# Places of a chunk without an edge: from a fetch of row 0 to no fetch, in a sparse graph-attention kernel

## The chip, the cores and the metric

The kernel runs on one core of one Trainium2 chip. The metric is the device time of one execution in microseconds (us). A second source is the hardware profile of one further execution, with every instruction, its waits and the packets of the DMA engines.

## The reference

Two layers of graph attention over 4096 nodes with 512 features. The adjacency is sparse: a random matrix of zeros and ones whose density falls with the index of both nodes, so that early nodes have many edges and late ones few. In this input there are 33,143 edges, and 15 nodes without any. Cut to what matters:

```python
# layer 0
h  = einsum('nf,kfp->knp', x, W);  f1, f2 = h . a_src, h . a_dst        # 8 heads of 64
e  = where(adj > 0, leaky_relu(f2[:, :, None] + f1[:, None, :], 0.2), -1e16)
x  = layernorm(x + concat_heads(softmax(e) @ h))
# layer 1: the same with 8 heads, elu, then the same with one head of 512, elu,
# then relu(out @ lin1_w + lin1_b) @ lin2_w + lin2_b
x  = layernorm(x + ...)
```

So attention is computed three times over the same edges: stage 0 (8 heads), stage 1 (8 heads) and stage 2 (one head of 512). A node without an edge gets the mean of all rows.

## The kernel before

**Edge search.** For each of 32 tiles of 128 nodes, `find_edges` reads the adjacency rows, finds the columns of the edges with VectorE's max operations, and writes them as a list of places. The places of one half of a tile (64 nodes) lie one after another, 128 to a chunk, one place on each partition. The number of chunks is fixed when the program is built, from the expected number of edges with a margin of 4.2 standard deviations; a pair is one chunk of each half. A place has three things: `idx`, the row to fetch (L926); `nl`, which of the 64 nodes it belongs to, or -1 if it holds no edge (L904); and its column in `s1`, from which TensorE spreads the node's score over the places. For a place without an edge, `idx` comes out as 0 and its column of `s1` as zeros. Tile 0 has four parts and more than 100 candidates a part and goes another way (L917 on). The blocks of `find_edges` are put in order by a scheduler; what follows is in an order written out by hand.

**Stages 0 and 1** (`heads_layer`) go over the tiles from 31 down to 0, in units of up to six chunks. `Attention.gather` issues one indirect DMA per chunk on GpSimd's queue (L987): each partition gets the table row (520 floats: features and a score for each head) that `idx` names. The gathers write into buffers `g` of six chunks; seven of these are in use (GB), so GpSimd runs seven units ahead and waits only for a buffer that TensorE has finished with. `spread` multiplies `s1` with the node's score split into three bf16 parts (L1013), and VectorE adds these up (L1022). `weights` adds the fetched score (L1052 to L1054) and takes the exponential on ScalarE, once in place in `g` (L1056) and once to scale the rows (L1059). `add` makes the selection matrix `sm` by comparing `nl` with 0 to 63 (L1080), scales the rows (L1111) and accumulates `sm` times rows on TensorE (L1102). A place with `nl` of -1 has an empty row in `sm`, so what it fetched counts for nothing. In the hand-written order, `weights` of the next unit stands before `add` of this one. When a tile is done it is normalised and projected to the next stage's table, which SP's queue writes to HBM (L681); at the end comes one more row, the mean (`finish_mean`, L740). The next stage's gathers wait for the whole table.

**Stage 2** has four buffers (GT), rows of 514 floats, the weight inside `sm` (L1089), and two dense layers (L1376, L1388) that are woven in between units by a fixed pace.

Lines that the text below touches: L904 (`nl`), L916 and L922 (`src`), L926 (`idx`), L852 to L875 (the degrees of a tile), L882 (`s1`), L987 (gather), L1009 to L1026 (scores), L1190 (first gathers of stages 0 and 1), L1326 (first gathers of stage 2).

Of the kernel before, what the change touches and what calls it, by code (L numbers as in the profile page):

```python
# [10 lines left out]
F32 = mybir.dt.float32  # L11
BF16 = mybir.dt.bfloat16
# [3 lines left out]
AF = mybir.ActivationFunctionType  # L16
OP = mybir.AluOpType
# [4 lines left out]
P = 128  # L22
N = 4096
F = 512
# [13 lines left out]
HS = 8  # L38
DM = 64
HN = P // 2  # L40
GC = 6
GB = 7
KW = 512
WIDE = 12
GT = 4

# [488 lines left out]
def sparse_path(  # L535
# [23 lines left out]
    nc = tc.nc  # L559
# [3 lines left out]
    total = sum(p.pairs for p in pts)  # L563
# [26 lines left out]

    idx = const.tile([P, total, 2], I32, name="idx")
    nl = const.tile([P, total, 2], F32, name="nl")
    s1 = const.tile([P, total * P], BF16, name="s1")

    class Stage2:
# [198 lines left out]
    def find_edges(big, sb, ps, pk, constants, sg, beside):  # L794
# [10 lines left out]
        for v, p in enumerate(pts):  # L805
# [89 lines left out]
            for lo in range(0, nch, per):  # L895
                m = min(per, nch - lo)
                pl = ps.tile([P, m, 2, k + 2], F32, name="pl")
                for c in range(m):
                    chunk = s1[:, (c0 + lo + c) * P : (c0 + lo + c + 1) * P]
                    nc.tensor.matmul(pl[:, c], chunk, rhs, start=True, stop=False)  # L900
                    nc.tensor.matmul(pl[:, c, :, : k + 1], chunk, rest, start=False, stop=False)
                    nc.tensor.matmul(pl[:, c, :, k:], ident_b, own_b, start=False, stop=True)
                cs = slice(c0 + lo, c0 + lo + m)
                nc.scalar.copy(nl[:, cs], pl[:, :, :, k + 1])  # L904
                src = sb.tile([P, most * 2], F32, name="src")[:, : 2 * m]
                sel = sb.tile([P, 512], F32, name="sel")[:, : m * 2 * k].rearrange("p (m h k) -> p m h k", k=k, h=2)
                if k < 100:
                    shape = [P, m, 2, k]
                    nc.vector.tensor_tensor(
                        sel,  # L910
                        iota_k[:, lo : lo + m, None, :k].to_broadcast(shape),
                        pl[:, :, :, k : k + 1].to_broadcast(shape),
                        op=OP.is_equal,
                    )
                    nc.vector.tensor_tensor(sel, sel, pl[:, :, :, :k], op=OP.mult)
                    nc.vector.tensor_reduce(src, sel.rearrange("p m h k -> p (m h) k"), AX.X, OP.add)  # L916
                else:  # L917
                    kk = sb.tile([P, most, 2], F32, name="kk")[:, :m]
                    nc.scalar.copy(kk, pl[:, :, :, k])
                    for c in range(m):  # L920
                        for h in range(2):
                            nc.vector.scalar_tensor_tensor(  # L922
                                sel[:, c, h], iota_k[:, lo + c, :k], kk[:, c, h : h + 1], pl[:, c, h, :k],
                                op0=OP.is_equal, op1=OP.mult, accum_out=src[:, 2 * c + h : 2 * c + h + 1],
                            )
                nc.gpsimd.tensor_copy(idx[:, cs].rearrange("p m h -> p (m h)"), src)  # L926
            if p.last:
                beside(t)
        limits = [big.tile([P, nv], F32, name=f"limits{i}") for i in range(2)]
# [46 lines left out]
    class Attention:  # L976
# [4 lines left out]
            self.s, self.ls, self.acc, self.den, self.seen = {}, {}, {}, {}, {}  # L981

        def gather(self, u):
            u.g = self.gp.tile([P, GC, F + HS], F32, name="g")
            for k in range(u.n):
                i, h = divmod(k, u.hn)
                nc.gpsimd.indirect_dma_start(  # L987
                    out=u.g[:, k, : self.st.row],
                    out_offset=None,
                    in_=self.st.table[:, :],  # L990
                    in_offset=bass.IndirectOffsetOnAxis(ap=idx[:, u.c0 + i, h : h + 1], axis=0),
                    bounds_check=N,
                    oob_is_err=False,
                )

        def spread(self, t):
# [5 lines left out]
            for name, of in (("s", self.s), ("ls", self.ls)):  # L1002
# [1 line left out]
                    [P, widest if wide else WIDE, 2, hs], F32, name=f"{name}{hs}",  # L1004
                    tag=f"{name}w" if wide else name, bufs=1 if wide else 3,
                )[:, :pairs]
            cuts = list(range(0, pairs, 10))

            def scores(lo):  # L1009
                pss = self.ps.tile([P, 10, 2, 3, hs], F32, name="pss")  # L1010
                m = min(10, pairs - lo)
                for i in range(m):
                    nc.tensor.matmul(  # L1013
                        pss[:, i].rearrange("p g a h -> p (g a h)"),
                        s1[:, ts(base + lo + i, P)],
                        st.s3[:, t].rearrange("p g a h -> p (g a h)"),
                        start=True, stop=True,
                    )
                return pss[:, :m]

# [153 lines left out]

        return rest

    def heads_layer(gp, wk, sb, pp, st, nxt, fetch, finish):

# [3 lines left out]
        with tc.tile_pool(name=f"ha_{st.name}", bufs=2, space=PSUM, reuse_waits="tile") as pacc, \  # L1184
# [2 lines left out]
                tc.manual_schedule():  # L1187
            at = Attention(st, gp, wk, pacc, one)
            extra = {}
            for u in units[:GB]:  # L1190
                at.gather(u)
            for t in order[:2]:
# [109 lines left out]

        return rest

    heads_layer(gp, wk, sb, pp, st0, st1, fetch0, finish0)
    heads_layer(gp, wk, sb, pp, st1, st2, lambda t: None, lambda o, t, _: elu(sb, o))


    layers.close()
    with tc.tile_pool(name="tg", bufs=GT, side="right", reuse_waits="tile") as gp, \  # L1310
# [12 lines left out]
        order = [t for block in blocks for t in block]  # L1323
        units = units_of(order)
        at = Attention(st2, gp, wk, pacc, ps)
        for u in units[:GT]:  # L1326
            at.gather(u)
        l1w = big.tile([P, FC, HID], F32, name="sl1w")
# [167 lines left out]
```

## Time and profile before

| | |
|---|---|
| median of six executions | 2272.0 us (2269.53 to 2275.16) |
| the profiled execution | 2275.27 us, of which the span of instructions is 2273.5 us |
| edge search, up to the first gather | 0 to 524 us |
| stage 0, first gather to first gather of the next | 524.3 to 1012.2 us |
| stage 1 | 1012.2 to 1497.4 us |
| stage 2 | 1497.4 us to the end |
| busy: TensorE, VectorE, ScalarE, GpSimd | 1741.7, 1362.3, 650.6, 1214.9 us |
| gathers | 1017, 1031.9 us busy on GpSimd, 1015 ns mean |
| DMA | 139,788 packets, 415.47 MB, of these 81,360 packets and 269.79 MB for the gathers |
| granted TensorE clock, mean | 0.895 |

Reading it: the busy time of a gather is GpSimd's own work on it; when the rows land is seen from what waits for them. A wait is listed under the engine and line that waited, with what released it. Shares over the whole span mix four phases with different limits, so the phases are looked at one by one.

### The profile page before, as it was taken

How to read it: one execution, taken by the hardware profiler on the slowest of the kernel's cores; microseconds unless marked ns; L12 is line 12 of the kernel's file. 1: busy time of each engine (PE TensorE's matmuls, PEld its weight loads, DVE VectorE, ACT ScalarE, POOL GpSimd, SP SyncE). 2: the span in 40 equal slices, each digit the busy share in tenths (PEclk: the TensorE clock that was granted, in tenths of full speed). 3: DMA queues.
4: the chain of work that ended last, by engine and by line, in shares of the span. 5: the costliest groups of instructions: out<-in, count | busy, mean ns of one | idle time of the engine just before them, and what ended most of it. 6: DMA issues, size and time to landing. Idle time of an engine off the chain costs nothing.

```text
span 2273.5 us, 29407 instructions
## 1 busy us (share of the span) xinstructions
PE 1741.7 (77%) x8935; PEld 1019.2 (45%) x8935; DVE 1362.3 (60%) x3744; ACT 650.6 (29%) x2354; POOL 1214.9 (53%) x1647
## 2 busy tenths in 40 slices
PE   3887876662887876756987767638989998898987
PEld 2665532221655553424655444325444444444444
DVE  5787777774989987736877667524242433424322
ACT  3346766560332221102433222012111111111111
POOL 5413333336777777727777777555547544444300
PEclk9899987785999997877999997869999999999998
DMA  6434555536998988727888888575556645544401
GB/s 213 126 112 162 201 202 219 216 118 169 282 276 275 276 260 235 222 80 213 234 224 224 224 216 216 156 214 162 148 152 189 187 127 150 159 129 145 134 19 43
DMA packets 139788, 415.47 MB, mean 183 GB/s; under 512 B 33819, under 2 KB 34851, under 8 KB 135654
## 3 DMA queue, kind: packets, MB, share of 16 engines
q0 software_dynamic: 81360, 269.79, 43.6%
q1 hardware_dynamic: 58262, 143.72, 18.0%
q8 instruction: 74, 1.21, 0.2%
q14 instruction: 92, 0.75, 0.1%
HBM read 371.18 MB, written 42.24 MB: 182 GB/s over the span
## 4 chain that ended last, share of the span: by engine, by line
PE 22%; DMA 13%; issue 13%; DVE 12%; POOL 9%; ACT 1%; POOLq 0%; DVEq 0%; SPq 0%; ACTq 0%
DMA g<-table_t,idx 11%; PE p L1376 10%; POOL g L987 9%; PE acc L1102 7%; DVE g L1111 4%; PE p L1388 3%; PE ph L667 2%; DMA xr<-sx_d 2%; DVE bs L1160 1%; DVE sm L1089 1%; DVE xr L1393 1%; DVE sm L1080 1%; DVE z L1053 1%; DVE z L1052 1%; DVE o L1139 1%
## 5 line engine op out<-in xcount | busy, mean ns | idle before, releaser
L987 POOL DMA_INDIRECT g<-table_t,idx x1017 | 1031.9, 1015 | 600.1 <-issue 296.4
L1102 PE MATMUL acc<-g,sm 128*64 128x260 f32 (+2 forms) x4068 | 602.6, 432 | 268.6 <-DVE g L1111 194.9
L1102 PEld LDWEIGHTS acc<-g,sm 128*64 128x64 f32 x4068 | 344.9, 153 | 498.9 <-DVE g L1111 253.7
L667 PE MATMUL ph<-sw_t,xt 128*128 128x264 f32 (+1 forms) x1536 | 392.0, 404 | 49.7 <-ACT xt L656 39.2
L1111 DVE TENSOR_TENSOR g<-g,wp 128x2048 f32<-128x2048 f32 (+4 forms) x148 | 383.2, 2589 | 10.6 <-ACT wp L1059 10.6
L667 PEld LDWEIGHTS ph<-sw_t,xt 128*128 128x128 f32 x1536 | 292.5, 197 | 114.3 <-ACT xt L656 55.4
L825 DVE MAX8 cand<-key 128x8 f32<-128x24 f32 (+54 forms) x467 | 196.7, 445 | 83.4 <-PE key L819 83.1
L1388 PE MATMUL p<-sl2w,shid 128*128 128x512 f32 x512 | 229.5, 602 | 0.0
L1376 PE MATMUL p<-sht,sl1w 128*128 128x512 f32 (+1 forms) x576 | 227.9, 551 | 0.0
L1052 DVE TENSOR_TENSOR z<-s,g 128x48 f32<-128x48 f32 (+6 forms) x222 | 40.8, 184 | 240.8 <-DMA g<-table_t,idx 231.5
L656 ACT ACTIVATE xt<-pt 128x128 f32<-128x128 f32 x384 | 101.4, 279 | 218.5 <-PE pt L653 217.9
L1376 PEld LDWEIGHTS p<-sht,sl1w 128*128 128x128 f32 x576 | 107.6, 191 | 110.4 <-issue 105.5
L1388 PEld LDWEIGHTS p<-sl2w,shid 128*128 128x128 f32 x512 | 96.0, 192 | 121.0 <-issue 120.5
L818 PE MATMUL key<-sg,s_identb 128*128 128x512 bf16 (+1 forms) x258 | 116.1, 451 | 30.1 <-DVE cand L825 25.5
L791 ACT ACTIVATE sg<-raw 128x4096 bf16<-128x4096 int32 (+1 forms) x39 | 116.9, 2998 | 9.8 <-PE key L818 5.0
L680 ACT COPY hrow<-ph 128x260 f32<-128x260 f32 (+2 forms) x194 | 70.7, 373 | 169.9 <-PE ph L667 169.9
L819 PE MATMUL key<-frac,places 128*128 128x512 bf16 (+1 forms) x258 | 116.7, 453 | 1.8 <-POOL places L754 1.8
L1379 ACT ACTIVATE shid<-p,sl1b 128x512 f32<-128x512 f32 (+1 forms) x72 | 46.1, 640 | 248.7 <-PE p L1376 248.7
L1089 DVE TENSOR_SCALAR sm<-iota_n,nl,w 128x64 f32<-128x64 f32 x339 | 83.8, 325 | 46.1 <-ACT w L1062 45.8
L1156 DVE SCALAR_TENSOR_TENSOR o<-ex,o 128x512 f32<-128x512 f32 x64 | 44.1, 689 | 100.3 <-ACT ex L1155 100.2
L1059 ACT ACTIVATE wp<-z 128x32 f32<-128x32 f32 (+4 forms) x148 | 30.6, 207 | 236.9 <-DVE g L1111 236.8
L852 POOL TENSOR_SCALAR degs<-balance 128x1 f32<-128x1 f32 x35 | 6.7, 192 | 141.8 <-ACT signs L850 137.3
(161 smaller groups left out, 1830.1 us busy)
## 6 DMA issues: line engine op xcount, KB each, us to landing
raw<-in_adj_dram SPq DMA_DIRECT2D x31, 2048.0 KB, 7.7
table_t<-hrow SPq DMA_DIRECT2D x64, 260.0 KB, 4.0
xr<-in_x_dram SPq DMA_DIRECT2D x64, 256.0 KB, 4.1
g<-table_t,idx POOLq DMA_INDIRECT x1017
table_t<-hrow SPq DMA_DIRECT2D x32, 257.0 KB, 5.5
sx_d<-o SPq DMA_DIRECT2D x32, 256.0 KB, 5.1
xr<-sx_d SPq DMA_DIRECT2D x32, 256.0 KB
out_dram<-xr SPq DMA_DIRECT2D x32, 256.0 KB, 3.0
```

Source lines behind the costliest of these rows:

```text
L656: nc.scalar.activation(xt[:, c, :], pt[:, c, :], AF.Copy, accum_out=st.xparts[:, c, t : t + 1])
L667: nc.tensor.matmul(ph[:n], columns(c), st.w[:, c, j], start=(c == 0), stop=(c == FC - 1))
L791: nc.scalar.activation(sg[:, ts(i, w)], raw[:, ts(i, w)], AF.Sign)
L818: nc.tensor.matmul(out_, ident_b, sg[:, j:e], start=True, stop=False)
L819: nc.tensor.matmul(out_, places[:, w], frac[:, j - w * KW : e - w * KW], start=False, stop=True)
L825: nc.vector.max(out=cand[:, at : at + 8], in_=part)
L987: nc.gpsimd.indirect_dma_start(out=u.g[:, k, : self.st.row], out_offset=None, in_=self.st.table[:, :], in_offset=bass.IndirectOffsetOnAxis ...
L1089: nc.vector.tensor_scalar(sm[:, k], iota_n, node[:, i, h : h + 1], u.w[:, k], op0=OP.is_equal, op1=OP.mult)
L1102: nc.tensor.matmul(out_[h * HN : (h + 1) * HN], sm[:, k], rows(k), start=flags[k][0], stop=flags[k][1])
L1111: nc.vector.tensor_mul(body, body, wp[:, :, :, None].to_broadcast(body.shape))
L1376: nc.tensor.matmul(p1, l1w[:, c, ts(k, P)], hts[b][:, c, :n], start=(c == 0), stop=(c == FC - 1))
L1388: nc.tensor.matmul(p2, hids[b][:, k, ts(j, P)], l2w[:, k, :], start=(k == 0), stop=(k == HC - 1))
```

## The change

A place without an edge gets a row number past the table's end: `past` is 8192 where `nl` is below -0.5 and 0 elsewhere, and is added to `src` before the cast to `idx`. The gather's bound is 4096 (`bounds_check=N`), and a row past it is to be left out without an error (`oob_is_err=False`); both were there before. What such a place finds in its buffer is then what was there earlier. So that this is a finite number, the buffers are filled with zeros once: seven passes of ScalarE ahead of stage 0's gathers, none for stage 1, which has the same buffers, and four memsets on GpSimd ahead of stage 2's gathers, whose buffers lie elsewhere in memory. So that the exponential stays finite as well, the score of such a place becomes -1e30: `hole` holds this value, and one more matmul per group of pairs puts it beside the three parts of the score, in a fourth column that VectorE's sum takes in. The sum less its own leaky value is then 0, and the weight 1. Groups of scores go from ten pairs to eight, so that a group with four parts still fits its PSUM tile.

```diff
+FAR = -1e30
+    hole = const.tile([P, total, 2], BF16, name="hole")
...
                 nc.scalar.copy(nl[:, cs], pl[:, :, :, k + 1])
+                nc.gpsimd.tensor_scalar(hole[:, cs], nl[:, cs], -0.5, FAR, op0=OP.is_lt, op1=OP.mult)
...
-                nc.gpsimd.tensor_copy(idx[:, cs].rearrange("p m h -> p (m h)"), src)
+                past = sb.tile([P, most * 2], F32, name="past")[:, : 2 * m]
+                nc.gpsimd.tensor_scalar(
+                    past, nl[:, cs].rearrange("p m h -> p (m h)"), -0.5, 2.0 * N, op0=OP.is_lt, op1=OP.mult
+                )
+                nc.gpsimd.tensor_add(past, past, src)
+                nc.gpsimd.tensor_copy(idx[:, cs].rearrange("p m h -> p (m h)"), past)
...
-            cuts = list(range(0, pairs, 10))
+            cuts = list(range(0, pairs, 8))
...
-                pss = self.ps.tile([P, 10, 2, 3, hs], F32, name="pss")
-                m = min(10, pairs - lo)
+                pss = self.ps.tile([P, 8, 2, 4, hs], F32, name="pss")
+                m = min(8, pairs - lo)
+                nc.tensor.matmul(
+                    pss[:, :m, :, 3, :], ident_b,
+                    hole[:, base + lo : base + lo + m, :, None].to_broadcast([P, m, 2, hs]),
+                    start=True, stop=True,
+                )
                 for i in range(m):
                     nc.tensor.matmul(
-                        pss[:, i].rearrange("p g a h -> p (g a h)"),
-                        s1[:, ts(base + lo + i, P)],
-                        st.s3[:, t].rearrange("p g a h -> p (g a h)"),
-                        start=True, stop=True,
+                        pss[:, i, :, :3, :], s1[:, ts(base + lo + i, P)], st.s3[:, t], start=True, stop=True
                     )
...
             at = Attention(st, gp, wk, pacc, one)
             extra = {}
+            if clear:
+                for _ in range(GB):
+                    g = gp.tile([P, GC * (F + HS)], F32, name="g")
+                    nc.scalar.activation(g, ones.to_broadcast(g.shape), AF.Copy, scale=0.0)
             for u in units[:GB]:
                 at.gather(u)
...
-    heads_layer(gp, wk, sb, pp, st0, st1, fetch0, finish0)
-    heads_layer(gp, wk, sb, pp, st1, st2, lambda t: None, lambda o, t, _: elu(sb, o))
+    heads_layer(gp, wk, sb, pp, st0, st1, fetch0, finish0, True)
+    heads_layer(gp, wk, sb, pp, st1, st2, lambda t: None, lambda o, t, _: elu(sb, o), False)
...
         at = Attention(st2, gp, wk, pacc, ps)
+        for _ in range(GT):
+            nc.gpsimd.memset(gp.tile([P, GC, F + HS], F32, name="g"), 0.0)
         for u in units[:GT]:
             at.gather(u)
```

## The prediction

> **What bounds the kernel now.** I read the page's busy shares and slices first, then busy time by stretch, then the gathers' group and the GpSimd waits, then GpSimd in order of time, then the DMA queues.
>
> ```profile
> POOL 5413333336777777727777777555547544444300
> DMA  6434555536998988727888888575556645544401
> ```
> The two rows of the 40 slices: from slice 11 (568 us) both GpSimd and the DMA engines are busy for most of the two eight-head stages, DMA more so. By stretch (busy us and count for each engine, clock, DMA share, GB/s):
>
> ```profile
> core 0: us, PE busy (x) PEld busy (x) DVE busy (x) ACT busy (x) POOL busy (x), PEclk, DMA share, GB/s
> 620.00:973.00 353.00, 273.07 (x1726) 178.13 (x1725) 301.25 (x585) 81.87 (x472) 267.80 (x266) 0.92 0.86 257
> 1064.00:1460.00 396.00, 309.38 (x1957) 205.05 (x1955) 288.51 (x492) 114.02 (x544) 304.83 (x300) 0.91 0.83 222
> 1497.00:2273.00 776.00, 672.93 (x2747) 352.07 (x2745) 269.29 (x978) 129.56 (x306) 343.49 (x339) 0.94 0.48 137
> ```
> No engine looks full in the first two; the third stage is TensorE's (673 of 776). What paces the first two shows only in GpSimd's waits (520 to 1480 us: releaser, us in total, times, longest):
>
> ```profile
> POOL g L987 <- issue: 213.9, 577, 37.6
> ```
> and in its order of time (start, us, what, idle before):
>
> ```profile
> 528.52 1.00 POOL L987 DMA_INDIRECT g<-table_t,idx  x1 [0.30 <-issue]
> 529.82 1.00 POOL L987 DMA_INDIRECT g<-table_t,idx  x1 [0.31 <-issue]
> ...
> 1459.79 1.00 POOL L987 DMA_INDIRECT g<-table_t,idx  x1 [0.30 <-issue]
> 1497.44 1.00 POOL L987 DMA_INDIRECT g<-table_t,idx  x1 [36.65 <-PE pss L1013]
> ```
> Each gather is 1.00 us of descriptor work and 0.30 us in which GpSimd waits for nothing shown. I took the distance of all neighbours: in both stages the median is 1.304 us, and only 10 of 338 (stage 0) and 15 of 338 (stage 1) exceed 1.5 us, 6.4 and 5.0 us of excess together. 338 x 1.304 = 441 us of the 449.3 and 447.6 us from first gather to last. So GpSimd's issue of gathers sets the pace of stages 0 and 1; DMA at 86% is a follower. In stage 2 gathers wait for TensorE to free buffers (213 us of waits on the accumulating matmuls there).
>
> ```profile
> q0 software_dynamic: 81360, 269.79, 43.6%
> ```
> All gathers: 81,360 packets are 1017 x 80, 64 of two rows and 16 completions of 4 B for every gather, whatever its places hold.
>
> From the inputs I counted the places: 339 gathers x 128 = 43,392 a stage, against 33,143 edges and 15 nodes without one. So 10,234 (23.6%) are empty; 42 gathers are empty throughout, 68 partly. All these fetch row 0, and the trace shows it: matching packets to gathers by order, a packet of a full gather takes 212 ns (stage 0) and 232 (stage 1), of an all-empty one 331 and 342; from end of issue to landing 3.2 and 3.0 us against 4.3 and 4.0. GpSimd's own time does not differ: 1.011 and 1.002 us in stage 0.
>
> **What the Trainium skill says.** "Perfetto Trace Analysis", DMA Instruction — SWDGE (GPSIMD): the profiled end of such a DMA is when the last DSP has generated descriptors, not when data has moved. The trace agrees: landing comes 3 us later. So the 1.00 us is generation, and fewer bytes don't shorten it. "DMA: Bandwidth & Descriptors", Why a DMA increments its semaphore by 16: for SWDGE all 16 engines post their count whatever the shape; the 16 small packets agree, so an empty gather still completes. "GPSIMD Engine Reference", 3.1: data-dependent branching costs about 12 cycles an element (10 ns at the page's 1.2 GHz). No run here shows what a row past the bound costs; that price is my upper end.
>
> **The change, part by part.** Sums are made against the profiled execution (2275.27 us, span 2273.5), which lies 3.3 us above the median of the six runs, 2272.0.
>
> 1. *Rows not fetched.* Per stage 10,234 x 2080 B = 21 MB less. In stages 0 and 1 this is hidden behind GpSimd's 1.304 us a gather: 0, if generation stays at 1.00 us. Unknown: the time of a place past the bound. Ends: nothing at all, -7.8 ns (1000/128), and +10 ns (the skill's branch). A gather has 30 such places on average. I take 0, since generation is one steady figure now (995 to 1000 ns for the 5th to 50th percentile) and the bound is already tested for every row.
>
> 2. *Earlier landing at the two stage ends*, which are on the path: after the last gather everything waits for it. The last unit of stages 0 and 1 holds 128, 128, 21 and 0 edges.
> ```profile
> 1460.52 2.28 DVE L1111 TENSOR_TENSOR g<-g,wp 128x2048 f32<-128x2048 f32 x1
> 1464.94 0.19 DVE L1052 TENSOR_TENSOR z<-s,g 128x32 f32<-128x32 f32 x1 [2.14 <-DMA g<-table_t,idx]
> ```
> The third gather's issue ends at 1459.47; plus 3.0 us it lands at 1462.5, VectorE is free at 1462.8 instead of starting at 1464.94: -2.1 us. At stage 0's end likewise 978.02 against 976.5: -1.5. I take -4 (-6 to -2).
>
> 3. *Stage 2.* Waits of z for gathers (86 us there) often stand at units that end in empty places, but around them the chain is TensorE's matmuls. TensorE's waits on sm after the start are 27 us (47.3 less the first, 20.3). I take -3 (-8 to 0).
>
> 4. *Clears in stage 2.* Four memsets of 128x3120 stand on GpSimd ahead of its first gather. GpSimd's iota of 128x1536 takes 1.417 us, 0.92 ns an element, its memset of 128x128 0.233: 2.9 us each. GpSimd idles from 1460.8 to 1497.4, so the first two, which wait for TensorE and VectorE, cost nothing (5.8 us if that gap were gone). The third lies over memory of stage 1's last rows: in the built program it carries the wait for all of SP's DMAs that the first gather carried. Those are:
> ```profile
> 1491.27 0.25 SPq L740 DMA_DIRECT2D table_t<-mrow  x1
> ```
> and the gather started at 1497.44 when that had landed. So two memsets come after it: 2 x 2.9 = +5.8 (5 to 7), and all gathers, and all of stage 2, shift.
>
> 5. *Clears in stage 0.* Seven ScalarE passes of 128x3120 ahead of the first gathers. ScalarE's last work before is
> ```profile
> 521.76 0.17 ACT L904 COPY nl<-pl 128x6 f32<-128x6 f32 x1 [1.36 <-PE pl L902]
> 536.63 0.24 ACT L1056 ACTIVATE g<-z 128x48 f32<-128x48 f32 x1 [14.70 <-DVE z L1054]
> ```
> Per element about 0.84 ns (128x4096 at 3.60 us, 128x128 at 0.28): 2.8 us each, the first ends at 524.7, the last at 541.5. The first gather started at 524.30: +0.4. The next buffers are needed 7.8 us apart: hidden. The first exponentials move from 536.6 to 541.5; VectorE's first multiply follows z of the second unit, whose gathers land at 544.2: hidden, with 2.5 us to spare; beyond that the consumers start late, and seven buffers (55 us) lie between them and GpSimd.
>
> 6. *Edge search.* 58 blocks gain three GpSimd operations, 0.22 + 0.22 + 0.19 us by neighbouring rows: 36.5 us of GpSimd, which is a third busy there. The two on nl are queued ahead of the next tile's degs, which wait 137 us in total for ScalarE's signs: hidden. The add stands between VectorE's src and idx; in half the tiles degs come right behind idx, and behind degs TensorE (56 us of its weight loads' waits are for deg): 16 x 0.3 = +4 to 5. I take +4, from 0 to 12, a third of it all.
>
> 7. *Hole scores.* 38 more matmuls with weight loads per stage, and reductions over four parts instead of three: about 0.05 us each on VectorE. Hidden in stages 0 and 1 (TensorE 77%, VectorE 73 to 85%); in stage 2 38 x 0.05 = +2 (1 to 4).
>
> Sum: 0 - 4 - 3 + 5.8 + 0.4 + 4 + 2 = **+5 us**: 2280 for a profiled execution, **2277** against the median.
>
> **Rivals.** *Generation gets shorter*: a place past the bound writes no descriptor. For it: 7.8 ns a row is a loop's price, and a skipped store is work saved. Against: a branchless ring of fixed length costs the same. At half of 7.8 ns: -40 us a stage. VectorE caps it: 301 of 353 us busy in stage 0's stretch, 289 of 396 in stage 1's; I take -25 and -40, with the sum +5: 2212. It ends on the faster side, and decides once a place saves over 0.5 ns (20,468 x 0.5 = 10 us). *Generation gets longer*: a place past the bound leaves the fast path. At 3 ns, +61 us: 2338; at 10 ns, +205: 2482. *Rows past the bound are fetched all the same*: parts 2 and 3 vanish, 2284.
>
> **How the numbers follow.** The chances: likeliest 0.52, longer 0.24, shorter 0.20, fetched anyway 0.04. The likeliest alone lies in 2268 to 2287. Within 0.2% (4.5 us, about what a measurement of this kernel can tell) it splits: 0.05 faster, 0.22 same, 0.25 slower. Shorter gives 0.18 faster and 0.02 slower, longer and fetched 0.28 slower: 0.23, 0.22, 0.55. The range leaves out half of "shorter" below 2225 and half of "longer" above 2350.
>
> **What would show it.** Distance of gathers still 1.304 us in stages 0 and 1, all-empty gathers at 1.00 us: step 1; another figure there decides for a rival. Fewer packets on q0, some 15,000 of 81,360 (30,702 rows, two to a packet). First gather of stage 2 some 12 us after the mrow write is issued instead of 6.2, with two memsets between: step 4. z after the last gather without its 2.14 us wait: step 2. First gather of stage 0 within 5 us of 524.3: steps 5 and 6. The prediction is wrong if GpSimd's time on gathers with empty places moves, which outweighs all else.

## The result and the profile after

The changed kernel takes 2275.0 us (median of 34 executions, 2267.92 to 2283.3) against 2270.1 us for the kernel before (71 executions in the same comparison): a ratio of 1.0022, 95% interval 1.0015 to 1.0029, 4.9 us more. The prediction was +5 us. The sum was right, but by luck: two of its seven terms were far off, in opposite directions, as the experiments below show.

The profiled execution of the changed kernel took 2272.28 us (span 2270.5), 3 us *less* than the profiled execution before, although the medians stand 4.9 us the other way. A single profile thus carries several us of chance, and readings of it are good for places and mechanisms, not for 2 us. The slices, by tenths of a fortieth of the span:

```profile
POOL 5514444346777777727777777565546545444400
DMA  6434555534777776625666667455345534434301
```
GpSimd stands as before, the DMA engines fell from 8 and 9 tenths to 6 and 7. Busy time by stretch, with the same columns and the same three stretches as before:

```profile
core 0: us, PE busy (x) PEld busy (x) DVE busy (x) ACT busy (x) POOL busy (x), PEclk, DMA share, GB/s
620.00:973.00 353.00, 276.12 (x1747) 180.99 (x1746) 303.45 (x588) 81.81 (x472) 268.29 (x266) 0.90 0.72 211
1064.00:1460.00 396.00, 315.20 (x2001) 207.96 (x2003) 294.38 (x500) 116.15 (x552) 304.61 (x302) 0.91 0.67 177
1497.00:2273.00 776.00, 674.22 (x2779) 357.42 (x2779) 271.10 (x980) 129.26 (x306) 343.48 (x340) 0.94 0.39 110
```
DMA share goes from 0.86 to 0.72, from 0.83 to 0.67 and from 0.48 to 0.39, and GpSimd issues exactly as many gathers in the first stretch, 266: its own pace did not move. The queue of the gathers on the page:

```profile
q0 software_dynamic: 81360, 206.30, 34.0%
```
63.5 MB less, and the *same number of packets*. By size, the trace has 33,126 packets of 4160 B and 16,563 of 4112 B, 96 of one row, 16,272 of 4 B (the completions), and 15,303 of 8 B, which take 8.3 ns each on average where one of 4160 B takes 247. A pair of two places past the bound is thus not left out: it becomes an 8-byte packet. The prediction had looked for some 15,000 packets fewer.

GpSimd in order of time, at the starts of stages 0 and 2 (start, us, what, idle before and its releaser):

```profile
525.44 0.20 POOL L934 TENSOR_TENSOR past<-past,src 128x6 f32<-128x6 f32 x1 [0.79 <-DVE ls L1048]
525.71 0.19 POOL L935 CAST idx<-past 128x6 int32<-128x6 f32 x1
527.56 1.32 POOL L997 DMA_INDIRECT g<-table_t,idx  x1 [1.66 <-DMA xr<-in_x_dram]
529.18 1.00 POOL L997 DMA_INDIRECT g<-table_t,idx  x1 [0.30 <-issue]
...
1457.53 1.00 POOL L997 DMA_INDIRECT g<-table_t,idx  x1 [0.30 <-issue]
1458.53 2.71 POOL L1344 MEMSET g<- 128x3120 f32 x1
1486.58 2.70 POOL L1344 MEMSET g<- 128x3120 f32 x1 [25.34 <-PE ph L669]
1491.98 5.34 POOL L1344 MEMSET g<- 128x3120 f32 x2 [2.70 <-DMA table_t<-mrow]
1497.47 1.01 POOL L997 DMA_INDIRECT g<-table_t,idx  x1 [0.15 <-POOL g L1344]
```
A gather still costs 1.00 us of GpSimd and 0.30 us up to the next. Over all neighbours the median distance is 1.304 us in stage 0 and 1.305 in stage 1, as before, and a fit of GpSimd's time over the number of empty places gives -0.05 ns a place in stage 0 and +0.04 in stage 1, no more than scatter. Stage 0's first gather starts 3.3 us later than before. Ahead of stage 2, two memsets follow the landing of `mrow`, as predicted; the second one waits for TensorE and stands at 1486.58, which matters below.

The starts of the stages in the two profiles:

| | before | after |
|---|---|---|
| first gather of stage 0 | 524.3 | 527.6 |
| stage 0, first to last gather | 449.3 | 450.1 |
| last gather to first of stage 1 | 38.6 | 36.3 |
| stage 1, first to last gather | 447.6 | 443.6 |
| last gather to first of stage 2 | 37.7 | 39.9 |
| from there to the end | 776.1 | 773.1 |

### The profile page after: what moved, and what is told of

It is laid out like the page before. It is cut to its first block, busy times and chain, and to the rows that moved or that the text cites. A ratio compares the mean times of both kernels' runs of the same rounds, so it can differ in the third digit from the quotient of the medians.

```text
span 2270.5 us, 29845 instructions
## 1 busy us (share of the span) xinstructions
PE 1754.2 (77%) x9049; PEld 1030.4 (45%) x9049; DVE 1370.4 (60%) x3750; ACT 669.9 (30%) x2361; POOL 1261.7 (56%) x1816
## 4 chain that ended last, share of the span: by engine, by line
PE 20%; issue 16%; DVE 12%; POOL 12%; DMA 11%; ACT 1%; POOLq 0%; DVEq 0%; SPq 0%; ACTq 0%
POOL g L997 12%; DMA g<-table_t,idx 10%; PE p L1395 8%; PE acc L1115 6%; DVE g L1124 4%; PE p L1407 3%; PE ph L669 2%; DMA xr<-sx_d 1%; DVE bs L1173 1%; DVE sm L1093 1%; DVE o L1152 1%; DVE z L1066 1%; DVE z L1065 1%; DVE sm L1102 1%; DVE z L1067 0%
## 5 line engine op out<-in xcount | busy, mean ns | idle before, releaser
L669 PE MATMUL ph<-sw_t,xt 128*128 128x264 f32 (+1 forms) x1536 | 396.9, 408 | 47.7 <-ACT xt L658 36.4
L658 ACT ACTIVATION_READ_ACCUMULATOR xt<-pt 128x1 f32 x384 | 80.0, 208 | 0.0
```

Of the source, the lines that this page charges most:

```text
L658: nc.scalar.activation(xt[:, c, :], pt[:, c, :], AF.Copy, accum_out=st.xparts[:, c, t : t + 1])
L669: nc.tensor.matmul(ph[:n], columns(c), st.w[:, c, j], start=(c == 0), stop=(c == FC - 1))
```

## The experiments

Eleven further kernels were run, one of them twice. Not tried was to issue nothing at all for the wholly empty gathers of the changed kernel. Each set below is compared with runs of the kernel before on the same chip.

### Set 1: what skipping is worth, and what the added work costs

**All rows fetched again.** The changed kernel with all its added work, but the number added for an empty place is 0:

```diff
-                    past, nl[:, cs].rearrange("p m h -> p (m h)"), -0.5, 2.0 * N, op0=OP.is_lt, op1=OP.mult
+                    past, nl[:, cs].rearrange("p m h -> p (m h)"), -0.5, 0.0, op0=OP.is_lt, op1=OP.mult
```


> The changed kernel in all but one number: a place without an edge gets row 0 again, so all rows are fetched and every added instruction stays. By the prediction's sum the rows left out are worth 7 us (4 at the ends of stages 0 and 1, 3 in stage 2), so this run is 12 us slower than the kernel before (+0.5%) and 7 slower than the changed one. Rival, that nothing waits for the relief because GpSimd's issue paces everything: equal to the changed kernel, +5 us. Rival, that the relief is large and the added work eats it: +25 us or more.

Measured: 2293.4 us against 2270.8, ratio 1.0096 (1.008 to 1.0111). This lies between the 12 us that were expected and the 25 or more of the second rival. So the added work costs 22.6 us, not the 12.2 that the prediction's steps 4 to 7 sum to, and leaving out the rows is worth 22.6 - 4.9 = 17.7 us, not 7, each give or take 3 or 4 us by the intervals. Two errors of 10 us each cancel. Where, by the profiles:

| | before | rows fetched again | after |
|---|---|---|---|
| first gather of stage 0 | 524.3 | 527.3 | 527.6 |
| stage 0, first to last gather | 449.3 | 459.8 | 450.1 |
| to the first of stage 1 | 38.6 | 36.8 | 36.3 |
| stage 1 | 447.6 | 449.6 | 443.6 |
| to the first of stage 2 | 37.7 | 43.5 | 39.9 |
| to the end | 776.1 | 776.2 | 773.1 |

Other kernels of this set show how far chance goes here. The next two (search alone, memsets alone) have the stages 0 and 1 of the kernel before: stage 0 takes 449.4 and 449.3 us in them, stage 1 446.0 and 445.4. The last one (clears on ScalarE) has those of the changed kernel: 453.2 and 444.5 us. So the added work stretches stage 0 by some 10 us, and skipping gives back 7 to 10 there and 5 to 6 in stage 1, where the prediction had put 0: the two stages in which a steady 1.304 us of GpSimd was to hide all of it. The last two columns differ by 22.6 us in all, 5 more than the medians' 17.7, which is the chance of single profiles.

The waits of GpSimd from 520 to 1010 us (us in total, times, longest) show how it does not. Before:

```profile
POOL g L987 <- PE acc L1102: 6.3, 6, 2.2
```
Rows fetched again:

```profile
POOL g L997 <- PE acc L1115: 16.6, 11, 5.3
```
After:

```profile
POOL g L997 <- PE acc L1115: 5.2, 4, 4.3
```
In the second profile of the changed stage 0 it is 10.1 us. GpSimd paces the stage only while TensorE has freed a buffer of the seven. Here the consumers are close behind: VectorE works 71.5 of 80 us from 580 to 660 us in the kernel before and 76.0 after. When the consumers are held, the ring fills, GpSimd stops, and what it loses it can't make up, since it has no slack of its own.

What holds them is in VectorE's waits of the same window. Before:

```profile
DVE z L1052 <- DMA g<-table_t,idx: 40.0, 11, 12.2
...
DVE s L1022 <- PE pss L1013: 11.7, 4, 6.0
```
Rows fetched again:

```profile
DVE z L1065 <- DMA g<-table_t,idx: 38.2, 9, 13.1
DVE s L1035 <- PE pss L1029: 19.2, 6, 8.7
```
After:

```profile
DVE z L1065 <- DMA g<-table_t,idx: 32.5, 9, 11.1
DVE s L1035 <- PE pss L1029: 19.2, 6, 8.7
```
The row that grew with the added work and did not shrink with skipping is the scores'. A tile of many pairs is summed in groups, and for every group but the last VectorE waits *in line*, since the sum (L1035) follows the matmuls at once in the hand-written order. With ten pairs to a group there were two such waits over 1 us in stage 0, of 4.8 and 6.0 us; with eight there are three, of 2.7, 8.7 and 6.3 us. The first is new, in the tile of nine pairs; most of the rest of the growth is the wait of the tile of twelve pairs, which was there before and got 4 us longer. In the same stretch, from the 240th to the 300th gather of stage 0, the gathers fall behind a beat of 1.305 us by 0.4, 2.5 and 1.0 us in the three profiles with the old scores, by 9.9 us with rows fetched again, and by 4.6 and 8.8 us in the two with rows left out. So the loss here comes with the added work; whether skipping takes any of it back, the scatter does not tell. Ahead of that (60th to 120th gather) it is 5.4, 3.0 and 3.8 us with the old scores, 5.5 with rows fetched again, and 1.3 and 0.5 with rows left out: there it is the landing of rows that skipping relieves, not the added work.

**The edge search alone.** The kernel before with the three GpSimd operations for each block, the added number 0, nothing else:

```diff
+                nc.gpsimd.tensor_scalar(hole[:, cs], nl[:, cs], -0.5, -1e30, op0=OP.is_lt, op1=OP.mult)
...
-                nc.gpsimd.tensor_copy(idx[:, cs].rearrange("p m h -> p (m h)"), src)
+                past = sb.tile([P, most * 2], F32, name="past")[:, : 2 * m]
+                nc.gpsimd.tensor_scalar(
+                    past, nl[:, cs].rearrange("p m h -> p (m h)"), -0.5, 0.0, op0=OP.is_lt, op1=OP.mult
+                )
+                nc.gpsimd.tensor_add(past, past, src)
+                nc.gpsimd.tensor_copy(idx[:, cs].rearrange("p m h -> p (m h)"), past)
```


> The kernel before with the three added GpSimd operations of each block of the edge search and nothing else; the added number is 0, so all rows are fetched and nothing later changes. By the sum: +4 us (0 to 12), in the time to the first gather. Rival, that GpSimd's share of a third leaves room for all of it: 0. Rival, that all 36 us lie on the chain from tile to tile: +36.

Measured: 2276.7 us, ratio 1.0028 (1.0017 to 1.0039), +5.9 us by the medians: within the prediction's 0 to 12, near its 4. The profile bears out only a part of it: the first gather starts at 525.8 us, against 523.6 in the next kernel of the same set, which has the old search.

**The memsets alone.** The kernel before with the four memsets ahead of stage 2:

```diff
+        for _ in range(GT):
+            nc.gpsimd.memset(gp.tile([P, GC, F + HS], F32, name="g"), 0.0)
```


> The kernel before with the four memsets ahead of stage 2's gathers and nothing else. By the prediction +5.8 us, with the stalled cast of VectorE +7; the first gather of stage 2 waits for two memsets after the rows of the table have landed. Rival, that the landing of the table and not the memsets sets the start (6.2 us from issue to first gather in the kernel before): +1 us or less.

Measured: 2277.0 us, ratio 1.0026 (1.0012 to 1.004), +6.2 us by the medians for the +5.8 predicted. GpSimd in order of time there:

```profile
1457.95 2.72 POOL L1327 MEMSET g<- 128x3120 f32 x1
1488.36 2.70 POOL L1327 MEMSET g<- 128x3120 f32 x1 [27.70 <-PE ph L667]
1493.92 5.34 POOL L1327 MEMSET g<- 128x3120 f32 x2 [2.86 <-DMA table_t<-hrow]
1499.41 1.01 POOL L987 DMA_INDIRECT g<-table_t,idx  x1 [0.16 <-POOL g L1327]
```
From the last gather to this one are 42.5 us, against 37.7 before. The two last memsets are the price, as reckoned. But the second, which the prediction put at nothing since GpSimd idles, is not free either. VectorE in order of time, in the changed kernel:

```profile
1487.25 2.07 DVE L702 CAST s_t<-s 128x16 bf16<-128x16 f32 x1
1489.35 0.19 DVE L703 TENSOR_TENSOR s<-s,s_t 128x16 f32<-128x16 f32 x1
```
and in the kernel before:

```profile
1489.75 0.18 DVE L700 CAST s_t<-s 128x16 bf16<-128x16 f32 x1
1489.97 0.19 DVE L701 TENSOR_TENSOR s<-s,s_t 128x16 f32<-128x16 f32 x1
```
The same cast takes 0.18 us, or 2.07 when the second memset runs (1486.58 to 1489.28), and ends with it at 1489.32. Over all profiles of this document, it takes 2.07 us in each of the six with that memset, and 0.18 in each of the eight without it. The Trainium skill has a rule for this in "SBUF — State Buffer", Summary: rules for kernel authors: when VectorE is in its two-port mode beside GpSimd, the second of the two to issue blocks until the first is done. That the cast ends with the memset agrees; that it runs in this mode the trace does not show. Through this cast goes the way to `mrow`, and with it to the first gather. In the changed kernel the delay was covered by another one that went away: the third memset, which waits for `mrow`, starts 1.3 us after its issue, while before the first gather started 6.2 us after it. Before, `mrow` was issued (1491.27 us) while the dense layers' weights were still coming in, and the packets of SP's queue ran on without a gap to 1496 us; in the changed kernel these loads were issued 5 us earlier and their packets had ended at about 1490, ahead of `mrow` (1490.64).

**Three of the clears on ScalarE.** The changed kernel with the last three clears of stage 2 done by ScalarE:

```diff
-        for _ in range(GT):
-            nc.gpsimd.memset(gp.tile([P, GC, F + HS], F32, name="g"), 0.0)
+        nc.gpsimd.memset(gp.tile([P, GC, F + HS], F32, name="g"), 0.0)
+        for _ in range(GT - 1):
+            g = gp.tile([P, GC * (F + HS)], F32, name="g")
+            nc.scalar.activation(g, ones.to_broadcast(g.shape), AF.Copy, scale=0.0)
```


> The changed kernel with three of stage 2's four clears on ScalarE, and only the first, whose memory is free early, on GpSimd. Theory: the changed trace shows two memsets (5.3 us) between the landing of the mean row and the first gather, and a third one under which VectorE's cast of the scores (L702) takes 2.07 us instead of 0.18, on the way to the mean row: 5.3 + 1.9 = 7 us are won, the kernel ends at 2 us below the one before (-0.1%), the cast is back at 0.2 us and the first gather of stage 2 starts some 7 us earlier. Rival, that the table's rows land only when the loads of the dense weights (4 MB ahead of them on SP's queue) are through, so that the memsets were covered: within 2 us of the changed kernel, +5 us on the one before.

Measured: 2273.0 us, ratio 1.001 (1.0001 to 1.002). Its cast takes 0.18 us, and 34.3 us pass from the last gather of stage 1 to the first of stage 2, against 39.9 after. The median shows some 2 to 3 of these 5.6 us, and the intervals of the two kernels overlap. The expected end 2 us below the kernel before did not come.

Steps 4 and 6 thus explain 12 of the 22.6 us, and 10.5 are left for the ScalarE clears and the scores, for which the prediction had 2.4. As each of the three measured numbers has an interval of about 3 us to either side, the 10.5 are good to some 5 us.

### Set 2: which row, the ScalarE clears, the scores

This set ran on another chip, and so did sets 3 and 4, on two more. There the kernel before takes 2452, 2430 and 2435 us instead of 2271. With the old search (third kernel of this set) the first gather starts at 523.5 us, as on the first chip, so the difference lies after it, and TensorE is where it comes from. The kernel before with ScalarE clears on the chip of set 2, TensorE's matmuls in order of time:

```profile
560.76 0.38 PE L1102 MATMUL acc<-g,sm 128*64 128x260 f32 x1 [1.52 <-issue]
562.90 0.59 PE L1102 MATMUL acc<-g,sm 128*64 128x260 f32 x1 [1.76 <-issue]
565.68 0.59 PE L1102 MATMUL acc<-g,sm 128*64 128x260 f32 x1 [2.19 <-issue]
567.78 0.59 PE L1102 MATMUL acc<-g,sm 128*64 128x260 f32 x1 [1.51 <-issue]
```
One matmul in two us or more, waiting for nothing that the profile shows, for some 20 us, and again in shorter stretches; on the first chip all 24 of a unit took 2.85 to 4.87 us here. The records grant TensorE 0.57 of its clock from 557 to 580 us, against 0.85 in the kernel before on the first chip; which of idling and clock causes the other they do not show. GpSimd then waits 114 us for TensorE's accumulation over stages 0 and 1, against 7 us in the kernel before on the first chip, and from first to last gather these stages take 532.6 and 525.8 us. Why these chips hold TensorE so is not known from the records. What can be carried from them is their own ratio; they say little about a stage that GpSimd paces.

**Another row at the empty places.** All the added work, and an empty place fetches the row of its own partition's number:

```diff
+    lane = const.tile([P, 1], F32, name="lane")
+    nc.gpsimd.iota(lane, [[0, 1]], base=0, channel_multiplier=1, allow_small_or_imprecise_dtypes=True)
...
-                    past, nl[:, cs].rearrange("p m h -> p (m h)"), -0.5, 2.0 * N, op0=OP.is_lt, op1=OP.mult
+                    past, nl[:, cs].rearrange("p m h -> p (m h)"), -0.5, lane, op0=OP.is_lt, op1=OP.mult
```


> The changed kernel with all its added work, but a place without an edge now fetches a row again: the row with the number of its own partition (0 to 127), where the kernel before and the previous run (all rows fetched, row 0 at every such place) fetched row 0. Theory A: skipping pays because row 0 read over and over is slow (packets of 331 to 342 ns against 212 to 232 in the kernel before), so spreading the reads gives most of the 17 us back although all bytes are moved: 2277 to 2282, ratio 1.003 to 1.005, packets of all-empty gathers near 230 ns. Theory B: skipping pays because 21 MB a stage less are moved: 2290 to 2295, ratio 1.0085 to 1.0105, as with row 0.

Measured: 2481.0 us against 2452.4, ratio 1.0105 (1.0077 to 1.0133); and in set 3, on the next chip, expected:

> Once more the changed kernel with a fetch of the own partition's row at every empty place, since on the chip of the first try TensorE was held back in stages 0 and 1 and the kernel before took 2452 us. Theory A (row 0 read over and over is what is slow): ratio 1.003 to 1.006. Theory B (bytes): ratio 1.0085 to 1.0105, as with row 0.

2449.1 against 2430.5, ratio 1.0086 (1.0054 to 1.0117). Both lie in the range of theory B or at its edge, and outside that of theory A. But no kernel with all the added work fetched row 0 on these chips, so this rests on a sum. In set 2, 28.6 us were measured; 17 us for the scores on this chip (below) and 5.9 and 6.2 us for search and memsets on the first make 29, which leaves nothing that distinct rows gave back. The packets say that row 0 was indeed slow. Mean time of a packet in stage 0, full gathers and wholly empty ones: 212 and 331 ns before, 228 and 312 ns in the next-but-one kernel (row 0, this chip), 239 and 234 ns here. With distinct rows the empty gathers are as fast as the full ones, but the full ones got slower too: the packets of all gathers together keep each of the 16 DMA engines busy for 325.7 us in stage 0 and 344.9 in stage 1 (on average), against 332.1 and 342.1 with row 0 on this chip. Leaving the rows out brings this down from 320.5 and 346.9 to 251.9 and 270.5 on the first chip. So the slow reading of the hot row is shown, and that it costs time in the whole is not.

**The same without any of the added work.**

```diff
-                nc.gpsimd.tensor_copy(idx[:, cs].rearrange("p m h -> p (m h)"), src)
+                nc.vector.scalar_tensor_tensor(
+                    idx[:, cs].rearrange("p m h -> p (m h)"), nl[:, cs].rearrange("p m h -> p (m h)"),
+                    lane, src, op0=OP.mult, op1=OP.max,
+                )
```
(`lane` is here minus the partition's number.)

> The kernel before, but a place without an edge fetches the row of its own partition number instead of row 0, by one VectorE operation for each block that replaces GpSimd's copy of the row numbers: nothing is skipped, nothing is cleared, no hole scores. All rows are finite, and their places have a zero column in the one-hot matrix, so the output stays. Theory A (row 0 is slow): 2256 to 2264, ratio 0.994 to 0.997. Theory B (bytes): 2268 to 2274, ratio 0.999 to 1.0015.

Measured: 2462.0 us, ratio 1.0043 (1.0027 to 1.0058): slower, and outside both expectations. The first gather of stage 0 starts at 535.9 us, 12.4 us later than in the next kernel on the same chip; the loss is no larger than this delay. From that gather to the end (the median less its start) it takes 1926 us, and the next kernel, with row 0, 1928: distinct rows win some 2 us, if anything, where theory A had 8 to 16. Why the search ends so late was not pursued, and it can't be the VectorE operation as such, since the last kernel below has the like of it and starts at 526.1.

**The ScalarE clears alone.** The kernel before with the seven clears ahead of stage 0's gathers:

```diff
+            if st is st0:
+                for _ in range(GB):
+                    g = gp.tile([P, GC * (F + HS)], F32, name="g")
+                    nc.scalar.activation(g, ones.to_broadcast(g.shape), AF.Copy, scale=0.0)
```


> The kernel before plus the seven ScalarE clears ahead of stage 0's gathers alone. The prediction took 0.4 us (hidden): ratio 1.000 to 1.0005. Theory: the first exponentials and all consumers of stage 0 start some 6 us later, GpSimd finds its buffers full more often in a stage whose gathers it paces, and part of the delay stays: +3 to +7 us, ratio 1.0015 to 1.003.

Measured: 2451.5 us, ratio 0.9988 (0.997 to 1.0006). No cost, as the prediction had it; the theory of 3 to 7 us falls, on this chip.

**The fourth part of the scores alone.** The kernel before with groups of eight, the added matmul (of zeros) and sums over four parts, which is the change's own edit of `spread`:

```diff
-            cuts = list(range(0, pairs, 10))
+            cuts = list(range(0, pairs, 8))
...
-                pss = self.ps.tile([P, 10, 2, 3, hs], F32, name="pss")
-                m = min(10, pairs - lo)
+                pss = self.ps.tile([P, 8, 2, 4, hs], F32, name="pss")
+                m = min(8, pairs - lo)
```


> The kernel before plus the scores' fourth part alone: groups of 8 pairs instead of 10, one more matmul a group that adds a part, here all zeros (cleared once), and reductions over four parts instead of three. Nothing is skipped or cleared. The prediction took +2 us, ratio 1.0005 to 1.0015. Theory: 22 us of added work less 6.4 (edge search) less 5.9 (clears of stage 2), less the ScalarE clears, stay for it: +3 to +6 us, ratio 1.0015 to 1.003.

Measured: 2469.6 us, ratio 1.0076 (1.0048 to 1.0104), some 17 us on this chip, where TensorE is scarce. Stage 0 takes 545.8 us from first to last gather, against 532.6 with the ScalarE clears alone; 8 of these 13 us lie between the 240th and the 270th gather, where set 1 had found the loss. The place is a weak sign on these chips: over sets 2 to 4 the gathers fall behind there by 10 to 14 us in four profiles with groups of ten, and by 14 to 20 in three with groups of eight. With the clears at nothing, the scores are what was left over.

### Set 3: is GpSimd's issue the pace?

The kernel before, but the 42 wholly empty gathers of a stage are plain loads on SP's queue:

```diff
+                if (u.c0 + i, h) in EMPTY:
+                    nc.sync.dma_start(u.g[:, k, : self.st.row], self.st.table[:P, :])
+                    continue
                 nc.gpsimd.indirect_dma_start(
```


> The kernel before, but the 42 gathers of each stage whose 128 places are all empty in this input are done as plain loads of 128 table rows on SP's queue: as many bytes, 42 fewer GpSimd gathers a stage (the list of gathers is fixed for this input, so this is a measurement and no kernel for other edges). Theory (GpSimd's issue of 1.304 us a gather sets the pace of stages 0 and 1): 42 x 1.304 = 55 us less in each, capped by VectorE, busy for 301 of 353 us in stage 0: 2170 to 2210, ratio 0.955 to 0.973, if TensorE is not held back as on the chip of the four runs before. Rival (DMA at 86% sets the pace): 2262 to 2275, ratio 0.997 to 1.002.

Measured: 2377.6 us against 2430.5, ratio 0.9764 (0.9737 to 0.9792). The bytes are the same, and 53 us are gone, so the number of GpSimd's gathers does count, even where TensorE is held. (The loads also read rows 0 to 127 in place of row 0; by set 2 that alone wins little or nothing.) The ratio lies between the two expectations, just short of the theory's, which was for a chip where TensorE is not held. The gain is about half of the 110 us that 2 x 42 x 1.304 us come to: 508 and 487 us from first to last gather, against 535 and 516 in the other kernel of this set, which carries the added work (the kernel before was not profiled on this chip). The rest turned into waits for buffers (GpSimd, 524 to 1620 us, waiting for the accumulation):

```profile
POOL g L991 <- PE acc L1106: 188.3, 50, 11.4
```
in the kernel with loads on SP's queue, against 108.8 us in the other. So once GpSimd is quicker, it waits more often for TensorE to free a buffer, on this chip.

### Set 4: the change without what it paid

**Groups of ten again.** The changed kernel, with the holes added into the three parts that were there, so that no fourth is needed:

```diff
-            cuts = list(range(0, pairs, 8))
+            cuts = list(range(0, pairs, 10))
...
-                pss = self.ps.tile([P, 8, 2, 4, hs], F32, name="pss")
-                m = min(8, pairs - lo)
+                pss = self.ps.tile([P, 10, 2, 3, hs], F32, name="pss")
+                m = min(10, pairs - lo)
                 nc.tensor.matmul(
-                    pss[:, :m, :, 3, :], ident_b,
-                    hole[:, base + lo : base + lo + m, :, None].to_broadcast([P, m, 2, hs]),
-                    start=True, stop=True,
+                    pss[:, :m].rearrange("p m g a h -> p m g (a h)"), ident_b,
+                    hole[:, base + lo : base + lo + m, :, None].to_broadcast([P, m, 2, 3 * hs]),
+                    start=True, stop=False,
                 )
...
-                        pss[:, i, :, :3, :], s1[:, ts(base + lo + i, P)], st.s3[:, t], start=True, stop=True
+                        pss[:, i], s1[:, ts(base + lo + i, P)], st.s3[:, t], start=False, stop=(i == m - 1)
```


> The changed kernel, but the hole scores are accumulated into the three parts that were there before (one matmul of the identity with the holes opens each group, the pairs' matmuls add to it), so that a group holds 10 pairs again and the reductions three parts; a hole then scores -3e30 instead of -1e30, which gives the same weight. Theory (what the hole scores cost is not the added work but the smaller groups: every further group of a tile of many pairs makes VectorE wait in line 6 to 9 us for its matmuls, once more in stage 0 and once or twice more in stage 1): 7 to 12 us less than the changed kernel, 2263 to 2268 on a chip where the kernel before takes 2271, ratio 0.997 to 0.999; VectorE waits two times over 1 us for the scores in stage 0, not three. Rival (the added matmul and its operand are what costs): 2273 to 2276, ratio 1.001 to 1.0025. On a chip where TensorE is held back: ratio 1.000 to 1.004 against 1.008 for the hole scores alone there.

Measured: 2429.8 us against 2434.8, ratio 0.9982 (0.9966 to 0.9998), a little below even the ratio expected for such a chip. This kernel still has the added matmul and takes back the smaller groups and the fourth part together; since what skipping is worth on this chip was not measured, the number does not say which of them costs. The waits that it was to take away can't be counted here: with TensorE held, VectorE waits for scores eight times over 1 us in stage 0.

**And the rest made smaller.** Groups of ten, ScalarE for three of stage 2's clears (as in set 1), and in the search

```diff
-                nc.gpsimd.tensor_scalar(hole[:, cs], nl[:, cs], -0.5, FAR, op0=OP.is_lt, op1=OP.mult)
...
-                past = sb.tile([P, most * 2], F32, name="past")[:, : 2 * m]
-                nc.gpsimd.tensor_scalar(
-                    past, nl[:, cs].rearrange("p m h -> p (m h)"), -0.5, 2.0 * N, op0=OP.is_lt, op1=OP.mult
-                )
-                nc.gpsimd.tensor_add(past, past, src)
-                nc.gpsimd.tensor_copy(idx[:, cs].rearrange("p m h -> p (m h)"), past)
+                nc.vector.scalar_tensor_tensor(
+                    idx[:, cs].rearrange("p m h -> p (m h)"), nl[:, cs].rearrange("p m h -> p (m h)"),
+                    -2.0 * N, src, op0=OP.mult, op1=OP.max,
+                )
...
+        nc.vector.tensor_scalar(hole, nl, 0.0, -FAR, op0=OP.min, op1=OP.mult)
```


> The kernel of the run before this one, and the rest of the added work made smaller: the row numbers by one VectorE operation a block (the larger of the source and -8192 times the node number) in place of three GpSimd ones and a copy, the holes by one VectorE operation at the end of the edge search, and three of the four clears of stage 2 on ScalarE. If the terms measured so far add up (skipping -17, groups -9 of the added 22, edge search -4 to -6, clears -3): 2255 to 2262 on a chip where the kernel before takes 2271, ratio 0.993 to 0.9965. Rival (the VectorE operation in the search costs as much as GpSimd's three, VectorE being the busier there): 2261 to 2267. On a chip where TensorE is held back: ratio 0.996 to 1.001.

Measured: 2425.3 us against 2434.8, ratio 0.9967 (0.995 to 0.9984): faster than the kernel before, by 9.5 us. Its operations in the search, by group (busy us, mean ns, idle before):

```profile
L928 DVE SCALAR_TENSOR_TENSOR idx<-nl,src 128x4 int32<-128x4 f32 (+6 forms) x55 | 8.5, 154 | 0.0
L934 DVE TENSOR_SCALAR hole<-nl 128x362 bf16<-128x362 f32 x1 | 0.3, 343 | 0.0
```
8.8 us of VectorE in place of four groups on GpSimd that take 49.8 us in the changed kernel. The changed kernel itself was not run on this chip; that this version also beats it (1.0022) rests on a comparison across chips, and the intervals of the two kernels of this set overlap.

## Why the prediction was right, and where it was not

The total of +5 us and its side were right; the rivals with a shorter or a longer generation are out, and so is the one in which the rows are fetched all the same. That the total came out within 0.1 us is luck: the gain was 11 us larger than forecast and the cost 10 us.

- **What bounds the kernel.** GpSimd's issue as the pace was right as far as it goes: the distance stayed at 1.304 us, and 42 gathers less a stage gave 53 us, on a chip where TensorE is held. It was wrong to conclude that nothing else reaches the end. The 6.4 us of excess that were set aside as small are the sign of a ring that runs full at times.
- **Step 1, rows not fetched: 0 in stages 0 and 1.** GpSimd's time did not move, as said. But rows that land earlier free TensorE and VectorE earlier, and GpSimd's waits for buffers drop from 16.6 us in stage 0 to 5.2 in one profile and 10.1 in another: 7 to 10 us there and 5 to 6 in stage 1. This is the term that failed most: the gain of the whole of steps 1 to 3 was 17.7 us, not 7.
- **Step 2, the ends: -4.** 0.5 us at stage 0's end and 3.6 at stage 1's, with and without the fetch. The mechanism was right and its sign was not: `z` still waits for its gather. VectorE at the end of stage 1 with rows fetched again, and after:

```profile
1478.22 0.19 DVE L1065 TENSOR_TENSOR z<-s,g 128x32 f32<-128x32 f32 x1 [2.19 <-DMA g<-table_t,idx]
1459.75 0.19 DVE L1065 TENSOR_TENSOR z<-s,g 128x32 f32<-128x32 f32 x1 [1.81 <-DMA g<-table_t,idx]
```

The last gathers start at 1473.38 and 1457.53 us, so `z` follows after 2.2 us instead of 4.8, and at stage 0's end after 2.3 instead of 4.7. VectorE gets to `z` sooner as well, which is why it still waits.

- **Step 3, stage 2: -3.** 776.2 against 773.1 us.
- **Step 4, memsets: +5.8.** 6.2 measured alone, with two memsets after the landing. The second memset, said to be free, holds a cast of VectorE by 1.9 us. The sign "12 us from the issue of `mrow` to the first gather" came out as 6.8, since `mrow` was there 1.3 us after its issue.
- **Step 5, ScalarE clears: +0.4.** Nothing measurable, on one of the chips with TensorE held.
- **Step 6, search: +4.** 5.9 measured. The trace has 55 blocks, not 58, and the three added operations take 39.3 us in them, not 36.5.
- **Step 7, scores: +2, "hidden in stages 0 and 1".** This failed by about 10.5 - 2.4 = 8 us. I had priced the operations, 0.05 us each, and not the groups: from ten pairs to eight puts one more in-line wait over 1 us of VectorE into stage 0 and makes another longer (19.2 us of waits for scores instead of 11.7), where VectorE has little to spare. That it is the size of the groups rather than the added matmul or the fourth part is argued from the place and the waits; the kernel that sets the matmul apart ran only where TensorE is held.
- **Fewer packets on the gathers' queue** was wrong: as many packets, 15,303 of them of 8 bytes.

Whether skipping helps by the bytes or by the hot row is not settled. What there is speaks for the bytes: on the chips of sets 2 and 3 a fetch of distinct rows was no better, and it left the gathers' packet time as it was. On the first chip, where skipping was measured, it was not run.

## What to carry to other kernels

An engine with a steady beat paces a stage only while its buffers come free; before putting a saving in another resource at nothing, look at the excess over the beat and at who releases it. When an edit makes a tile's group smaller, count the waits that stand in line between groups, not only the instructions (they are the likely cost here, not a proven one). And a forecast whose gains and costs are each wrong by the same amount looks right: put the edit back in halves, one run with all the cost and none of the gain, before believing the sum.

## What the runs showed of the hardware

- A row past the bound of an indirect DMA is still described: the gather takes 1.00 us of GpSimd with 128 such rows as with none, and each pair of them goes out as one packet of 8 bytes, 8.3 ns.
- One row read over and over is slow: 331 ns a packet in wholly empty gathers of stage 0 against 212 in full ones on the first chip, 312 against 228 on the second; with distinct rows there 234 against 239.
- A memset on GpSimd held a VectorE cast of 128x16 from f32 to bf16 for 2.07 us instead of 0.18, up to the memset's end, in six profiles of six.
- The same kernel took 2271 us on one chip and 2430 to 2452 us on three others, on the first of these (profile with the ScalarE clears) with TensorE issuing single matmuls 2 to 3 us apart for some 20 us early in stage 0, at a granted clock of 0.57 against 0.85.
